# Layer 3 of a four-layer sequence: B from DRAM instead of TensorE, dt x spread in PSUM, C in banks of its own

## The chip, the cores and the metric

The kernel runs on one core of one Trainium2 chip. The metric is the device time of one launch in microseconds (us); lower is better. All arithmetic is float32.

## The reference, cut to what matters

Four layers follow one another on an image of 2 x 128 x 64 x 64: a two-way Mamba scan (layer 0), two attention layers (1 and 2), and the layer that is changed here. Layer 3 reads the 128 channels of each of the 8192 pixels as a short sequence of 8 tokens with 16 features, and runs a small Mamba over it (32 inner channels, 16 states), then a group norm, a Silu and a residual:

```python
seq = x.transpose(0, 2, 3, 1).reshape(B * H * W, 8, 16)
xi, z = split(seq @ in_proj_w.T, 2)              # 32 + 32 inner channels
xs = silu(causal_conv4(xi) + conv_b)
dt, Bm, Cm = split(xs @ x_proj_w.T, [1, 17])     # 1, 16 and 16 columns
dt = softplus(dt @ dt_proj_w.T + dt_proj_b)
dA = exp(dt[..., None] * A)
dBx = dt[..., None] * Bm[:, :, None, :] * xs[..., None]
h = dA_t * h + dBx_t                             # over the 8 tokens
y = (sum over states of h * C_t) + xs * D
xr = (y * silu(z)) @ out_proj_w.T
out = x + silu(group_norm(xr) * gamma + beta)
```

## The kernel before

The whole program is written out in order by hand, in one manual schedule per layer; every engine then runs its own queue in that order, waiting on semaphores only. Layer 3 begins at line 1090.

**Tiling.** The 2 x 4096 pixels are cut into 16 chunks of T = 512 pixels (eight for each image). Within a chunk the partitions hold 4 tokens x 32 inner channels, so two groups (index `i`) hold the 8 tokens; row block `j` of 32 partitions is one token. For the recurrence each token is spread out: partition 32 n + d holds channel d with four of the 16 states, and the remaining four groups `g` of states lie along the free axis. `PLACE` (line 39) tells in which `(i, j)` the two tokens of a step lie: a chunk takes four steps `k`, each with two tokens `o` = 0, 1. The first token of step 0 needs no decay and the last token of step 3 no state.

**What a step computes.**
- `dtr` (line 1216): dt of a token, spread over the states by transfers. The chunk's `put` writes dt and dt x to DRAM (`ddt`, `ddx`), and `spread(k)` reads them back with four transfers of 64 KB a token, into `dtr` and `rx`.
- `da_` (1253): A = exp(dt a), four ScalarE instructions, one for each `g`.
- `db_` (1245): TensorE spreads B over the partitions through `spread_by` with the weights `lb`, one matmul of 32 x 128 for each token and `g`, into a tile `q`; VectorE multiplies by `rx` into D.
- `mul` and `add` (1260, 1266): the recurrence. GpSimd forms A h in place of A; the sum D + A is the new h, in halves of two `g`, three of four halves on VectorE and one on GpSimd (`todo`).
- `hc_` (1271): TensorE spreads C with the weights `lc` into `q`, VectorE multiplies A h by it; `y_` (1285) sums the states on TensorE, with `y0_` (1277) having begun the sum with xs D and the part C·B dt x.

**What a chunk computes beside that.** `xs_`, `sz_`, `dt_` (1173 to 1188): projections of 1024 columns, two matmuls into one `q`. `e_exp`, `e_ln` (ScalarE), `dt_add`, `dtx_` (GpSimd): softplus and dt x. `bc_`, `cbx_` (1221, 1231): C·B for each token, spread and multiplied into dt x. `yg_`, `xr_`, `bn_`: gate, output projection, statistics. After eight chunks `Norm` treats the first image beside the next chunks.

**What sets the order.** The main loop goes over steps s and, in each, over four units g. In the body, `hc_` is of step s-1, the recurrence (`advance`) of step s, and `db_`, `da_` of step s+1; `extra` names what is put in at (k, g), such as the next chunk's projections, all one chunk ahead. This is the middle of it:

```python
for g in range(4):
    if pc_ is not None:
        pc_.hc_(pk, g)
    if g == 0:
        advance()
    if nc_ is not None:
        nc_.db_(nk, g)
    if g and pc_ is not None:
        pc_.y_(pk, g - 1)
```

**Buffers.** [...]`q` is a pair of banks with three buffers, shared by B, C and all projections, and `y` has two. D and A have three buffers each of (128, 2, 4, 512), `dtr` and `rx` two. All transfers go through SP's queue, in program order.

Of the kernel before, what the change touches and what calls it, by code (L numbers as in the profile page):

```python
# [13 lines left out]
P = 128  # L14
B, C, H, W = 2, 128, 64, 64
L = H * W
T = 512
# [4 lines left out]
NHC, NH, NDBU = 4, 3, 3  # L22
ND = 73
# [33 lines left out]
def conv_seq_kernel(ctx: ExitStack, tc: tile.TileContext, a: dict, out: bass.AP):  # L57
# [1031 lines left out]
    with ExitStack() as c3:  # L1089
# [8 lines left out]
        def pq():  # L1098
            return ps.tile([P, 2, T], F32, tag="q", name="q", bufs=3)
# [27 lines left out]
        lb = gt([P, NS, 32], "lb", wp)  # L1127
        lc = gt([P, NS, 32], "lc", wp)
        nc.vector.tensor_copy(lb, _bc(xpT[:, 1:17], 2, [P, NS, 32]))
# [17 lines left out]
        for b in range(B):  # L1147
            nc.sync.dma_start(kept[b], x[:, b, :])
# [6 lines left out]
        class Chunk3:  # L1155
# [10 lines left out]
            def two(self, w, rhs):  # L1166

                self.p = pq()
                for i in range(2):
                    mm(self.p[:, i, :], lhsT=w[:, i * P : (i + 1) * P] if w.shape[1] > P else w,  # L1170
                       rhs=rhs(i), start=True, stop=True)

            def xs_(self):
                self.two(flat(lm), lambda i: x[:, self.b, self.sl])
                self.xs = wt("xs", bufs=3)
                act(self.xs, self.p, AF.Silu, bias=v("cb3"))

            def sz_(self):
                self.two(flat(lz), lambda i: x[:, self.b, self.sl])
                self.sz = wt("sz", bufs=3)  # L1180
                act(self.sz, self.p, AF.Silu)

            def dt_(self):
                self.two(flat(ldt), lambda i: self.xs[:, i, :])
                self.e = wt("e")
                self.dt = wt("dt", bufs=1)
                act(self.e, self.p, AF.Abs, bias=v("bdt3"))
                nc.vector.tensor_scalar(self.dt, self.p, v("bdt3"), 0.0, ALU.add, ALU.max)
# [13 lines left out]
            def put(self):  # L1202
                self.ddt = dr.tile([P, 2, T], F32, tag="ddt", name="ddt")
                self.ddx = dr.tile([P, 2, T], F32, tag="ddx", name="ddx")
                nc.sync.dma_start(self.ddt, self.dt)
                nc.sync.dma_start(self.ddx, self.e)

            def spread(self, k):

                i, j = PLACE[k]  # L1210
                for what, src, toks in (("dtr", self.ddt, (1,) if k == 0 else (0, 1)),
                                        ("rx", self.ddx, (0,) if k == 3 else (0, 1))):
                    t = wt(what)
                    for n in range(4):
                        for o in toks:
                            nc.sync.dma_start(t[32 * n : 32 * n + 32, o, :],  # L1216
                                              src[32 * (j + o) : 32 * (j + o) + 32, i, :])
                    getattr(self, what)[k] = t


            def bc_(self):
                self.p = pq()
                for j in range(2):
                    for i in range(2):
                        mm(self.p[64 * i : 64 * i + 64, j, :], lhsT=flat(wbc[:, j]),
                           rhs=self.xs[:, i, :], start=True, stop=True)
                self.bs = wt("bs", (P, T), bufs=1)
                nc.scalar.copy(self.bs, self.p[:, 0, :])
                nc.vector.tensor_mul(self.bs, self.bs, self.p[:, 1, :])

            def cbx_(self):
                self.two(flat(nsum), lambda i: self.bs)
                nc.vector.tensor_mul(self.e, self.e, self.p)


            def spread_by(self, w, k, g, toks):
                i, j = PLACE[k]
                q = pq()
                for o in toks:
                    r = slice(32 * (j + o), 32 * (j + o) + 32)  # L1240
                    mm(q[:, o, :], lhsT=flat(w[r, 4 * g : 4 * g + 4, :]), rhs=self.xs[r, i, :],  # L1241
                       start=True, stop=True)
                return q[:, toks[0] : toks[-1] + 1, :]

            def db_(self, k, g):
                toks = (0,) if k == 3 else (0, 1)
                if g == 0:
                    self.D[k] = wt("D", (P, 2, 4, T), bufs=3)
                q = self.spread_by(lb, k, g, toks)
                sl = slice(toks[0], toks[-1] + 1)  # L1250
                nc.vector.tensor_mul(self.D[k][:, sl, g, :], self.rx[k][:, sl, :], q)  # L1251

            def da_(self, k, g):
                sl = slice(1, 2) if k == 0 else slice(0, 2)
                if g == 0:
                    self.A[k] = wt("A", (P, 2, 4, T), bufs=3)
                act(self.A[k][:, sl, g, :], self.dtr[k][:, sl, :], AF.Exp,  # L1257
                    scale=aneg[:, 2 * NS + g : 2 * NS + g + 1])

            def mul(self, k, o, half):  # L1260
                g = slice(2 * half, 2 * half + 2)
                h = self.D[k][:, 0, g, :] if o else self.D[k - 1][:, 1, g, :]
                a_ = self.A[k][:, o, g, :]
                nc.gpsimd.tensor_mul(a_, a_, h)  # L1264

            def add(self, k, o, half, eng):
                g = slice(2 * half, 2 * half + 2)
                d = self.D[k][:, o, g, :]
                eng.tensor_add(d, d, self.A[k][:, o, g, :])  # L1269

            def hc_(self, k, g):
                toks = (1,) if k == 0 else (0, 1)
                q = self.spread_by(lc, k, g, toks)
                a_ = self.A[k][:, toks[0] : 2, g, :]
                nc.vector.tensor_mul(a_, a_, q)  # L1275

            def y0_(self, i):
                if i == 0:
                    self.y = {}
                self.y[i] = ps.tile([P, T], F32, tag="y", name="y", bufs=2)  # L1280
                for w, rhs in ((diag_d, self.xs), (ident, self.e)):
                    mm(self.y[i], lhsT=w, rhs=rhs[:, i, :], start=w is diag_d, stop=False,  # L1282
                       skip_group_check=True)

            def y_(self, k, g):
                i, j = PLACE[k]
                for o in (1,) if k == 0 else (0, 1):
                    r = slice(32 * (j + o), 32 * (j + o) + 32)
                    mm(self.y[i][r], lhsT=rep[:, 0:32], rhs=self.A[k][:, o, g, :], start=False,  # L1289
                       stop=(g == 3 and k % 2 == 1), skip_group_check=True)  # L1290


            def yg_(self, i):
                nc.vector.tensor_mul(self.sz[:, i, :], self.sz[:, i, :], self.y[i])

            def xr_(self):
                self.p = pq()
                for i in range(2):
                    mm(self.p[:, 0, :], lhsT=flat(lo[:, i]), rhs=self.sz[:, i, :],
                       start=(i == 0), stop=(i == 1))  # L1300
                nc.scalar.copy(x[:, self.b, self.sl], self.p[:, 0, :])
# [4 lines left out]
        class Norm:  # L1306
# [3 lines left out]
            def first(self):  # L1310
                self.mv = wt("mv", (P, 2), bufs=1)
                nc.vector.bn_aggr(self.mv, flat(stats[:, self.b]))
                self.p = pq()[:, 0, :]
                mm(self.p[:, 0:1], lhsT=gmean, rhs=self.mv[:, 0:1], start=True, stop=True)

            def second(self):
# [8 lines left out]
                self.p = pq()[:, 0, :]  # L1325
# [17 lines left out]
            def load_all(self):  # L1343
                t = wt("D", (P, 2, 4, T), bufs=3).rearrange("p a g t -> p (a g t)")
                nc.sync.dma_start(t, kept[self.b])
                for k in range(4):
                    self.xl[k] = t[:, 1024 * k : 1024 * k + 1024]
# [14 lines left out]

        def at(s):
            return steps[s] if 0 <= s < len(steps) else (None, 0)

        with tc.manual_schedule():
            c = chunks[0]
            c.xs_()
            c.sz_()
            c.dt_()  # L1370
            c.e_exp()
            c.e_ln()
            c.dt_add()
            c.dtx_()
            c.put()
            for k in range(2):
                c.spread(k)
            c.bc_()
            c.cbx_()
            norms = [Norm(b) for b in range(B)]  # L1380
            for s in range(-1, len(steps) + 3):
                (pc_, pk), (cc, ck), (nc_, nk) = at(s - 1), at(s), at(s + 1)
                ci, k = divmod(s, 4)
                fut = chunks[ci + 1] if s >= 0 and ci + 1 < len(chunks) else None
                old = chunks[ci - 1] if ci > 0 else None
# [25 lines left out]
                extra = {}  # L1411

                def more(key, *what):
                    extra.setdefault(key, []).extend(what)

                if cc is not None:
                    more((0, 0), lambda: cc.y0_(0))
                    more((0, 4), lambda: cc.spread(3))
                    more((2, 2), lambda: cc.y0_(1))
                    more((3, 1), lambda: cc.yg_(0))  # L1420
                if old is not None:
                    more((1, 1), lambda: old.yg_(1))
                if fut is not None:
                    f = fut
                    more((0, 2), f.xs_)
                    more((0, 3), f.sz_)
                    more((1, 1), f.dt_, f.e_exp, f.e_ln)
                    more((1, 2), f.bc_)
                    more((1, 3), f.dt_add, f.dtx_, f.put)
                    more((1, 4), lambda: f.spread(0))  # L1430
# [164 lines left out]
```

## Time and profile before

| | |
|---|---|
| device time, three runs | 6737.71, 6741.09, 6753.5 us (median 6741.09) |
| the profiled execution | 6743.73 us; its span from first to last instruction 6741.9 us |
| layer 0 / layers 1 and 2 / layer 3 (page's slices and timeline) | to about 3.5 ms / to about 5.63 ms / from 5629 to 6742 us |
| chunks of layer 3 | 64.8 to 65.5 us for most; 75.5 and 75.4 us for the two beside which the first image is normalised |
| a steady chunk, busy us | TensorE 58.5, VectorE 51.8, GpSimd 49.0, ScalarE 26.9; DMA share 0.26, 73 GB/s |

How to read the profile's rows: a row of the timeline gives start and duration, the engine (PE is TensorE, PEld its weight loads, DVE VectorE, ACT ScalarE, POOL GpSimd, SPq the sync engine's queue of transfers), the line, the operation, the tile written and those read. In brackets stands how long the engine sat idle before it and who released it. A row of the waits view names who waited for whom. A row of groups gives busy us in all and mean ns of one. A float32 matmul of 512 columns is recorded as two passes, so counts of TensorE are double those in the code.

### The profile page before, as it was taken

How to read it: one execution, taken by the hardware profiler on the slowest of the kernel's cores; microseconds unless marked ns; L12 is line 12 of the kernel's file. 1: busy time of each engine (PE TensorE's matmuls, PEld its weight loads, DVE VectorE, ACT ScalarE, POOL GpSimd, SP SyncE). 2: the span in 40 equal slices, each digit the busy share in tenths (PEclk: the TensorE clock that was granted, in tenths of full speed). 3: DMA queues.
4: the chain of work that ended last, by engine and by line, in shares of the span. 5: the costliest groups of instructions: out<-in, count | busy, mean ns of one | idle time of the engine just before them, and what ended most of it. 6: DMA issues, size and time to landing. Idle time of an engine off the chain costs nothing. (4 is left out here: it accounts for less than half of the span.)

```text
span 6741.9 us, 67309 instructions
## 1 busy us (share of the span) xinstructions
PE 5957.8 (88%) x20652; PEld 2794.8 (41%) x20652; DVE 5535.0 (82%) x4521; ACT 4446.2 (66%) x7658; POOL 5393.9 (80%) x2471
## 2 busy tenths in 40 slices
PE   8888888888888888888889999999999997888888
PEld 2222222222222222222238877787788883222222
DVE  7999999999999999999986665565566676787777
ACT  7887788877788777887765654554456554434343
POOL 6999999999999999999975665555566666777676
PEclk7888788877778778787779999999999998888898
DMA  6656665665566665566620000000000002222222
GB/s 183 146 149 158 162 151 145 148 153 145 142 157 152 155 151 140 147 156 151 154 73 1 5 3 1 1 1 1 1 1 13 1 1 64 75 69 72 88 73 73
DMA packets 354733, 616.78 MB, mean 91 GB/s; under 512 B 73785, under 2 KB 76226, under 8 KB 353858
## 3 DMA queue, kind: packets, MB, share of 16 engines
q1 hardware_dynamic: 353488, 610.44, 35.9%
q8 instruction: 162, 2.65, 0.2%
q14 instruction: 201, 1.65, 0.1%
q10 hardware_dynamic: 882, 2.04, 0.1%
HBM read 496.72 MB, written 115.47 MB: 91 GB/s over the span
## 5 line engine op out<-in xcount | busy, mean ns | idle before, releaser
L383 POOL TENSOR_TENSOR dbu<-dus,bs 128x1024 f32<-128x1024 f32 x1024 | 2458.0, 2437 | 100.1 <-DVE h L427 85.5
L427 DVE TENSOR_TENSOR_SCAN h<-da,hst,dbu 128x1024 f32<-128x1024 f32 x896 | 2090.7, 2340 | 93.5 <-ACT dbu L411 88.8
L396 ACT ACTIVATE da<-dts,aneg 128x512 f32<-128x512 f32 (+1 forms) x2048 | 1410.1, 689 | 343.8 <-DVE h L427 305.5
L923 POOL TENSOR_TENSOR sum<-sum,sc 128x1024 f32<-128x1024 f32 x384 | 906.3, 2360 | 492.3 <-ACT sc L918 488.6
L885 ACT COPY sc<-s 128x512 f32<-128x512 f32 x1024 | 597.7, 585 | 858.8 <-PE s L880 745.1
L892 DVE TENSOR_TENSOR mx<-mx,s 128x512 f32<-128x512 f32 x896 | 609.1, 680 | 546.8 <-ACT sc L885 545.5
L880 PE MATMUL s<-q,k 128*128 128x256 f32 x4096 | 1051.6, 380 | 6.6 <-DVE k L857 3.3
L450 PE MATMUL y<-hc,cst 128*32 128x512 f32 x4096 | 880.2, 755 | 196.0 <-DVE hc L439 176.1
L935 PE MATMUL av<-sc,v 128*128 128x256 f32 x4096 | 1049.4, 379 | 2.5 <-ACT sc L918 2.5
L439 DVE TENSOR_TENSOR hc<-h,pc 128x1024 f32<-128x1024 f32 x704 | 841.4, 1195 | 9.7 <-PE y L450 7.4
L880 PEld LDWEIGHTS s<-q,k 128*128 128x128 f32 x4096 | 776.6, 190 | 140.3 <-issue 29.0
L935 PEld LDWEIGHTS av<-sc,v 128*128 128x128 f32 x4096 | 768.6, 190 | 103.1 <-ACT sc L918 3.9
L437 POOL TENSOR_TENSOR hc<-h,cs 128x1024 f32<-128x1024 f32 x320 | 762.0, 2381 | 1.1 <-issue 1.1
L1264 POOL TENSOR_TENSOR A<-A,D 128x1024 f32<-128x1024 f32 x224 | 525.6, 2363 | 231.7 <-DVE D L1269 202.5
L416 PE MATMUL pc<-xd,sel 16*128 16x512 f32 x1024 | 708.1, 782 | 0.1
L915 DVE TENSOR_TENSOR sc<-sc,pm 128x1024 f32<-128x1024 f32 x512 | 620.1, 1212 | 0.9 <-PE pm L911 0.9
L918 ACT ACTIVATE sc<-sc 128x1024 f32<-128x1024 f32 x512 | 541.9, 1059 | 8.6 <-DVE sc L915 8.1
L1257 ACT ACTIVATE A<-dtr,aneg 128x1024 f32<-128x1024 f32 (+1 forms) x256 | 245.8, 1031 | 389.4 <-PE y L1289 374.0
L340 PE MATMUL misc<-xd,w_dt 9*128 9x512 f32 x504 | 371.3, 824 | 145.0 <-ACT x L479 79.6
L450 PEld LDWEIGHTS y<-hc,cst 128*32 128x32 f32 x4096 | 125.3, 120 | 852.9 <-DVE hc L439 414.5
L1241 PE MATMUL q<-xs,lb 32*128 32x512 f32 x896 | 332.1, 713 | 75.4 <-DVE D L1251 68.6
L411 ACT ACTIVATE dbu<-hst,dbu,df 128x1 f32<-128x1 f32 x896 | 337.9, 377 | 82.5 <-POOL dbu L383 60.2
(263 smaller groups left out, 7868.4 us busy)
## 6 DMA issues: line engine op xcount, KB each, us to landing
dts<-ddt SPq DMA_DIRECT2D x512, 256.0 KB, 5.5
dus<-ddu SPq DMA_DIRECT2D x512, 256.0 KB, 5.1
bs<-rows SPq DMA_DIRECT2D x1024, 64.0 KB, 4.8
cs<-rows SPq DMA_DIRECT2D x1024, 64.0 KB, 3.3
ddt<-dt SPq DMA_DIRECT2D x128, 256.0 KB, 2.0
ddu<-dtu SPq DMA_DIRECT2D x128, 256.0 KB, 4.0
dtr<-ddt SPq DMA_DIRECT2D x448, 64.0 KB, 2.0
rx<-ddx SPq DMA_DIRECT2D x448, 64.0 KB, 2.0
```

The source lines that it names most:

```text
L383: nc.gpsimd.tensor_mul(t, self.dus[q], _bc(self.bs[g], 1, [P, 2, T]))
L396: act(t[:, i, sl], self.dts[q][:, i, sl], AF.Exp, scale=an[:, g, 2 * q + i : 2 * q + i + 1])
L416: mm(t, lhsT=sel[32:48, 4 * g : 4 * g + 4, :].rearrange("p n d -> p (n d)"), rhs=self.xd[32:48, :], start=True, stop=True)
L427: nc.vector.tensor_tensor_scan(ho, ai, bi, init, ALU.mult, ALU.add)
L437: nc.gpsimd.tensor_mul(t, self.h[u], _bc(self.cs[gq(u)[0]], 1, [P, 2, T]))
L439: nc.vector.tensor_mul(t, self.h[u], _bc(self.pc[u // 2], 1, [P, 2, T]))
L450: mm(self.y[q // 2][r : r + 32, :], lhsT=sum4, rhs=self.hc[u][:, i, :], start=False, stop=(u % 8 >= 6), skip_group_check=True)
L880: mm(p[:, o, :], lhsT=j.k[m // 8][:, m % 8 * P : m % 8 * P + P], rhs=self.q, start=True, stop=True)
L892: nc.vector.tensor_max(self.mx, self.s[0][:, 0:2, :] if u == 1 else self.mx, self.p[u])
L915: nc.vector.tensor_sub(s, s, _bc(self.pm[:, :], 1, [P, 4, NQ]))
L923: nc.gpsimd.tensor_add(self.sum, self.s[0] if w == 1 else self.sum, self.s[w])
L935: mm(self.av, lhsT=self.job.v[m // 8][:, m % 8, :], rhs=self.s[u // 2][:, m % 4, :], start=(m == 0), stop=(m == 31))
```

## The change

- **B by transfers.** `b_` copies the chunk's B rows (which `bc_` already made for C·B) to SBUF and stores them in DRAM (`rows`, 256 KB). `load(k, o)` fills D of one token (128, 4, 512) with B by four transfers of 256 KB, each reading four rows and repeating them over 32 partitions. D is now allocated for each token, in six half-size buffers. The weights `lb` go.
- **dt x by TensorE.** `rx_(k, o)` spreads a token's dt x over the partitions with one matmul into a PSUM bank (two buffers), instead of by transfers; the store `ddx` and the transfers to `rx` go. `db_` multiplies D in place by that bank, repeated over two `g`, in two halves a token.
- **C alone.** `pc_` makes C's tile `q` (two buffers of two banks), one unit ahead of the `hc_` that uses it (`prepare`). Step 0 of a chunk takes two units of 1024 columns instead of four of 512.
- **Projections in halves.** `xs_`, `sz_`, `dt_`, `cbx_` work on 512 columns each, through one bank `misc`; `xs_`, `sz_`, `b_`, `dt_` and `e_exp` are put two chunks ahead, the rest of the chain one chunk ahead. dt's relu moves from VectorE to ScalarE. C·B dt x is written over dt, not over dt x. `y` has one bank.
- **Copies of x.** The copy of each image's x to `kept` moves from before the loop to step 1 of chunks 0 and 1.

The diff, cut to its core:

```diff
+ND3 = 6
...
-        def pq():
-            return ps.tile([P, 2, T], F32, tag="q", name="q", bufs=3)
+        def misc():
+            return ps.tile([P, T], F32, tag="misc", name="misc")
...
-        for b in range(B):
-            nc.sync.dma_start(kept[b], x[:, b, :])
...
+            def one(self, w, rhs):
+                p = misc()
+                mm(p, lhsT=w, rhs=rhs, start=True, stop=True)
+                return p
+
+            def xs_(self, i):
+                if i == 0:
+                    self.xs = wt("xs", bufs=3)
+                p = self.one(flat(lm)[:, i * P : (i + 1) * P], x[:, self.b, self.sl])
+                act(self.xs[:, i, :], p, AF.Silu, bias=v("cb3"))
...
+            def b_(self):
+                p = self.bc_(0)
+                self.bs = wt("bs", (P, T))
+                nc.scalar.copy(self.bs, p)
+                self.rows = dr.tile([P, T], F32, tag="rows", name="rows")
+                nc.sync.dma_start(self.rows, self.bs)
+
+            def c_(self):
+                self.pc = self.bc_(1)
+
+            def cb_(self):
+                self.cb = wt("cb", (P, T), bufs=1)
+                nc.vector.tensor_mul(self.cb, self.bs, self.pc)
+
+            def dt_(self, i):
...
+                p = self.one(flat(ldt), self.xs[:, i, :])
+                act(self.e[:, i, :], p, AF.Abs, bias=v("bdt3"))
+                act(self.dt[:, i, :], p, AF.Relu, bias=v("bdt3"))
...
+            def load(self, k, o):
+
+                if k == 3 and o:
+                    return
                 i, j = PLACE[k]
+                t = self.D[k, o] = wt("D", (P, 4, T), bufs=ND3)
+                r = 64 * i + 16 * (j + o)
+                src = self.rows[r : r + 16].rearrange("(g n) t -> n g t", n=4)
+                for n in range(4):
+                    nc.sync.dma_start(t[32 * n : 32 * n + 32], src[n].partition_broadcast(32))
+
+            def cbx_(self, i):
+                self.pcb = self.one(flat(nsum)[:, i * P : (i + 1) * P], self.cb)
+
+            def ecb_(self, i):
+                nc.vector.tensor_mul(self.dt[:, i, :], self.e[:, i, :], self.pcb)
+
+            def rx_(self, k, o):
...
+                q = self.rx[k, o] = ps.tile([P, T], F32, tag="rx", name="rx", bufs=2)
+                mm(q, lhsT=rep[r, :], rhs=self.e[r, i, :], start=True, stop=True)
+
+            def db_(self, k, o, half):
+                d = self.D[k, o][:, 2 * half : 2 * half + 2, :]
+                nc.vector.tensor_mul(d, d, _bc(self.rx[k, o], 1, [P, 2, T]))
...
+            def unit(self, k, u):
+
+                return [(1, 2 * u), (1, 2 * u + 1)] if k == 0 else [(0, u), (1, u)]
+
+            def pc_(self, k, u):
+                i, j = PLACE[k]
+                self.q = getattr(self, "q", {})
+                q = self.q[k, u] = ps.tile([P, 2, T], F32, tag="q", name="q", bufs=2)
...
                 if cc is not None:
-                    more((0, 0), lambda: cc.y0_(0))
-                    more((0, 4), lambda: cc.spread(3))
-                    more((2, 2), lambda: cc.y0_(1))
-                    more((3, 1), lambda: cc.yg_(0))
+                    more((1, 2), lambda: cc.y0_(0), at=first)
+                    more((3, 2), lambda: cc.y0_(1), at=first)
+                    more((3, 0), lambda: cc.yg_(0))
...
+                if fut2 is not None and s >= 0:
+                    more((2, 1), lambda: fut2.xs_(0))
+                    more((2, 2), lambda: fut2.xs_(1))
+                    more((2, 3), lambda: fut2.sz_(0))
+                if fut2 is not None:
+                    more((3, 0), lambda: fut2.sz_(1), at=first)
+                    more((3, 1), fut2.b_)
+                    more((3, 2), lambda: fut2.dt_(0))
+                    more((3, 3), lambda: fut2.dt_(1), fut2.e_exp)
                 if fut is not None:
...
+                    more((0, 0), fut.e_ln)
+                    more((0, 1), fut.c_)
+                    more((0, 2), fut.cb_, fut.dt_add, fut.dtx_)
+                    more((0, 3), fut.put)
+                    more((0, 3), lambda: fut.cbx_(0))
+                    more((1, 0), lambda: fut.ecb_(0), lambda: fut.cbx_(1))
+                    more((1, 1), lambda: fut.ecb_(1))
+                if 0 <= ci < B:
+                    more((1, 3), lambda: nc.sync.dma_start(kept[ci], x[:, ci, :]))
+                if n2 is not None:
+                    more((k, 1), lambda: n2.load(n2k, 0))
+                    more((k, 2), lambda: n2.load(n2k, 1))
+                    more((k, 3), lambda: n2.spread(n2k))
+                    more((k, 2), lambda: n2.rx_(n2k, 0), at=first)
+                if nc_ is not None:
+                    more((k, 0), lambda: nc_.rx_(nk, 1), at=first)
...
                 for g in range(4):
+                    if g < units:
+                        prepare()
+                    if g == 0 and older is not None and ok:
+                        older.y_(ok, 3)
+                    for f_ in first.get((k, g), []):
+                        f_()
+                    for u in sums.get(g, []):
+                        pc_.y_(pk, u)
+                    if g < units:
+                        pc_.hc_(pk, g)
+                    if nc_ is not None and nk != 3:
+                        nc_.db_(nk, g // 2, g % 2)
+                    elif nc_ is not None and g % 2 == 0:
+                        nc_.db_(nk, 0, g // 2)
                     if g == 0 and nc_ is not None:
-                        for gg in range(4):
-                            nc_.da_(nk, gg)
-                    if g in (1, 2):
+                        nc_.da_(nk)
+                    if g < 3:
                         advance()
                     for f_ in extra.get((k, g), []):
                         f_()
```

Here `n2` is the step after next (s+2), `fut2` the chunk after next, and `first` holds what goes ahead of a unit's sums.

## The prediction

> **What bounds the kernel now.** I read the page's slices first: the last seven carry layer 3 (5629 us to the end), and the diff touches nothing else. Then the windows view, cut at the load of the Silu table that opens each chunk of 512 tokens' work (columns: us, busy us of TensorE, its weight loads, VectorE, ScalarE, GpSimd, clock, DMA share, GB/s):
>
> ```profile
> 5794.77:5859.64 64.87, 58.50 (x206) 15.11 (x208) 51.83 (x47) 26.93 (x28) 48.97 (x21) 0.89 0.25 73
> 5859.64:5924.52 64.88, 58.52 (x206) 15.09 (x208) 51.86 (x47) 26.92 (x28) 48.99 (x21) 0.89 0.26 73
> ```
>
> A steady chunk takes 64.9 us and no engine fills it; TensorE is nearest. So the waits view of 5650 to 6740 us (engine and line that waited, for whom, us in total, times, longest):
>
> ```profile
> POOL A L1264 <- DVE D L1269: 202.5, 82, 8.4
> PEld q L1241 <- DVE D L1251: 173.5, 101, 7.8
> DVE A L1275 <- PE q L1241: 138.9, 100, 3.1
> ...
> PE q L1241 <- DVE D L1251: 90.2, 39, 7.0
> ...
> DVE D L1269 <- POOL A L1264: 45.8, 17, 5.8
> POOL dt L1197 <- ACT e L1194: 45.7, 15, 6.3
> ```
>
> TensorE and VectorE wait for each other: the three buffers of q are shared by B, C and the projections, B's matmul waits for VectorE's last product, and VectorE (138.9/16 = 8.7 us a chunk) waits for C's. GpSimd hangs behind: its product waits for VectorE's sum. ScalarE's largest wait, 374 us for y, is slack.
>
> A second limit shows in the timelines, VectorE first, then GpSimd (start, us):
>
> ```profile
> 6156.46 3.35 DVE L1269 TENSOR_TENSOR D<-D,A 128x1024 f32<-128x1024 f32 x1 [2.24 <-POOL A L1264]
> ...
> 6173.29 2.98 DVE L1269 TENSOR_TENSOR D<-D,A 128x1024 f32<-128x1024 f32 x1
> ```
> ```profile
> 6154.07 4.66 POOL L1264 TENSOR_TENSOR A<-A,D 128x1024 f32<-128x1024 f32 x2
> ...
> 6170.51 4.68 POOL L1264 TENSOR_TENSOR A<-A,D 128x1024 f32<-128x1024 f32 x2 [1.25 <-DVE D L1269]
> 6175.27 3.22 POOL L1269 TENSOR_TENSOR D<-D,A 128x1024 f32<-128x1024 f32 x1
> ```
>
> The sum issued at 6156.46 ends 1.1 us after GpSimd's products (6158.73); the one at 6173.29 ends 1.08 us after 6175.19, and GpSimd's next operation then takes 3.22 instead of 2.36 us. They take turns.
>
> **What the Trainium skill says.** "SBUF — State Buffer", section "SBUF: two separate sides": a VectorE operation with two SBUF inputs and a GpSimd operation hold one shared port pair exclusively; an operand from PSUM doesn't need it, nor do DMAs. The trace agrees: sums take 1.21 to 3.37 us, the products with q (L1251, L1275) never over 1.22. "TensorEngine Tiling (Array Packing)", "Key Properties": tiles run in parallel. Agrees: B and C in different rows overlap here (start, us):
>
> ```profile
> 6130.26 0.70 PE L1241 MATMUL q<-xs,lc 32*128 32x512 f32 x2
> 6130.27 0.70 PE L1241 MATMUL q<-xs,lb 32*128 32x512 f32 x2
> ```
>
> "TensorE: Matmul & The Clock Gate", Part 1: the clock drops after about 3.4 us of idling. Agrees: after 3.56 us idle at 6160.47 two passes last 2.07 us where back-to-back passes take 0.59.
>
> **The change, part by part, for one chunk.** One matmul of 512 columns is recorded as two passes, 0.98 us from start to start (L1170: two matmuls in 1.98); a pair in different rows or columns takes about 1.0 (L1289 x4: 6127.36 to the next at 6128.35).
>
> *TensorE.* Now C is 16 units (12 pairs, 4 singles), B 16, y 16; the rest is 5 x 1.95 (xs, sz, dt, B·C spread, output) + 2.9 (B and C rows, L1225) + 2 x 2.1 (y0) = 16.9. Laid end to end that is 64.9; the 58.5 busy say that 6.4 of B lie over C. The change removes B's 16 and adds 7 matmuls that spread dt x (nearest row: a single of L1241, 1.0). So 16 + 16 + 7 + 16.9 = 55.9. The gain is **2.6, not 9**. If three of the seven overlap C in other rows it is 53.
>
> *VectorE.* B x dt x becomes 14 products of 1024 by a spread PSUM row instead of 12 x 1.21 + 4 x 0.68. The layer has no such form; layer 0 has, at 1195 ns:
>
> ```profile
> L439 DVE TENSOR_TENSOR hc<-h,pc 128x1024 f32<-128x1024 f32 x704 | 841.4, 1195 | 9.7 <-PE y L450 7.4
> ```
>
> I take 1.21; the ends are 1.19 and 1.28 (L1188). 14 x 1.21 = 16.9 against 17.2; C's products likewise 16.9 against 17.3; dt's relu (1.28) moves to ScalarE; B·C's product splits, 1.36 for 1.21. Together -1.8: 51.8 becomes 50.
>
> *ScalarE.* Three 1024-wide reads of PSUM in halves and two relus: from the 0.58 of a 512-wide copy (L1228), +1.5 on 26.9. Nothing while the wait for y is its largest; but the projections now share one bank (misc), so a late ScalarE would stop TensorE. Table loads stay four a chunk.
>
> *GpSimd and the shared ports.* Work is unchanged, but exponent and logarithm come earlier, so the 45.7/15 = 3 us wait of L1197 goes; what is late next is VectorE's sum. Port time: 18 x 2.34 + 2.85 + 2.35 + 8 sums x 1.1 = 56.1 a chunk, before and after.
>
> *SP and DMA.* Issues stay 58 a chunk (28 for dt, 28 for dt x or B, 2 stores) at 0.45 us (x8 in 3.56). Bytes rise from 4.7 MB to 28 x 64 KB + 28 x 256 KB + 0.8 MB = 10 MB, or 165 GB/s. Layer 0 carries 140 to 183 GB/s at a DMA share of 0.6, with pieces of this size:
>
> ```profile
> dts<-ddt SPq DMA_DIRECT2D x512, 256.0 KB, 5.5
> ```
>
> B is asked for one step (about 15 us) before its product. Its six half-buffers come free as the preceding step ends, so I cost it at nothing; the cover is that step. SP waits in order: the store of dt waits for GpSimd, with spreads and B loads behind it, as today (14 us a chunk at L1205); ScalarE's exponent waits for the spread. Two waits are new: VectorE's B product for its tile's four transfers, with C's product and a sum queued behind it and TensorE and GpSimd waiting for those; and the product that overwrites dt, early in step 1, for dt's store, issued late in step 0 and landing in 2.6 us (DMA view, ddt<-dt of 512 KB). The second hides behind two products and a sum. The copies of x (2 MB, 6.3 us) move from the start to steps 1 and 5, where B loads queue behind them: 0 to 6 us each, taken as offset by the start they leave.
>
> *Order.* C is made one unit ahead in two banks, so VectorE no longer waits for the matmul it has just released. The compiled order then gives each of a chunk's four steps (TensorE, in us):
>
> step 0: C 5, y 4, dt x 2, C rows 1.45, one B·C spread 1: 13.4
> step 1: C 3, y 5, dt x 2, spread 1, y0 2.1, output 1.95: 15.0
> step 2: C 4, y 3, dt x 1, xs 2, one z 1: 11.0
> step 3: C 4, y 4, dt x 2, z 1, y0 2.1, B rows 1.45, dt 1.95: 16.5
>
> The ports: step 0 two products and a sum of GpSimd's (3 x 2.34), 5.2 for dt, one sum of VectorE's (1.1), 13.3; steps 1 and 2 five of GpSimd's and three sums, 15.0; step 3 five and one, 12.8. VectorE, at 1.13 a product from start to start, 1.9 a sum, 0.6 a small one: 11.5, 14.3, 13.1, 11.5. The largest of each sum to 59.9. Lookahead of one unit can't carry step 2's slack far into step 3; I add 0.5 for turns at the ports: **60.4 against 64.9**. Times 15 (the sixteenth chunk is split over a start and an end that gain nothing: the start puts three more matmuls ahead, the end is unchanged; -5 to +6) gives 68 us. 6741.9 - 68 = 6674 of span; 1.8 us lie around it, and the profiled run stands 2.6 above the median: 6673.
>
> **The rivals.**
> - *The full gain.* Steps smooth over and the ports alone bind, 57 a chunk: -7.9 x 16 = -126, 6615. For it: clocks near 0.97 when TensorE never idles (5470 to 5629 us). Against: ports 98% full.
> - *Nothing.* Product, sum, product of the recurrence already sets the time, and TensorE's waits only fill it: chunks of 64 to 65.5, 6727 to 6750. For: GpSimd's 202.5 us wait for sums. Against: those sums stand behind products that wait for TensorE.
> - *Slower: transfers.* As compiled, each transfer of SP waits for the one eight places before it, so 58 of mean landing time L need 58 L/8. At the 2 us of today's 64 KB that is 15 us; at 5.5, 40; **from L = 9 it exceeds 64.9**. At 10 a chunk takes 72.5: +7.6 x 16 = +122, 6863. For: layer 0's pieces land in up to 7.5 us, and B's tile holds four. Against: its median.
> - *It doesn't do what it says*: if B's product waits for its tile each time, TensorE's gap remains under another name; this is the transfers' case in small.
>
> **How the numbers follow.** Forecast 0.56 (58.5 to 63 a chunk, 6640 to 6711), full gain 0.13, nothing 0.11, slower 0.20. About 0.3%, 20 us, is what a measurement of this kernel can tell from no change; "nothing" gives 0.02 to faster, 0.07 to same and 0.02 to slower, and 0.01 of the forecast's tail goes to same. Faster 0.70, same 0.08, slower 0.22. The range 6610 to 6765 takes in forecast, full gain, nothing and the mildest of slower; beyond it lie about 0.05 below and 0.15 above.
>
> **What would show it.** Right: chunks near 60 us; VectorE's wait for C's matmul well under 2 us a chunk; TensorE busy about 56 at a clock over 0.92; sums still 1.9 on average or more; DMA share near 0.6; the 3 us wait of L1197's successor gone. Wrong: waits of VectorE's B product or ScalarE's exponent for DMAs of over 2 us a chunk, pieces landing in over 9 us, or GpSimd's wait for sums staying near 12 us a chunk.

## The result, and the profile after

The changed kernel takes 6790.75 us (median of 6 runs, 6786.51 to 6801.13) against 6739.23 for the kernel before in the same comparison: a ratio of 1.0079, 95% interval 1.0065 to 1.0092. It is slower by 0.8%; 6673, 1% faster than before, had been forecast.

Where the time went is read from two marks: GpSimd's last addition of the layers ahead (L958 before, L959 after), and ScalarE's copy of a chunk's result (L1301 before, L1325 after), one a chunk. These are the addition and the first copy before, then after:

```profile
5628.50 0.73 POOL L958 TENSOR_TENSOR x<-x,t 128x256 f32<-128x256 f32 x1 [4.15 <-ACT t L956]
5756.48 0.59 ACT L1301 COPY x<-q 128x512 f32<-128x512 f32 x1 [3.56 <-PE q L1299]
5623.71 0.73 POOL L959 TENSOR_TENSOR x<-x,t 128x256 f32<-128x256 f32 x1 [4.14 <-ACT t L957]
5793.27 0.59 ACT L1325 COPY x<-misc 128x512 f32<-128x512 f32 x1 [10.15 <-PE misc L1323]
```

The layers ahead are the same in all kernels, but end between 5616 and 5634 us in the profiles of this case, so layer 3 is timed from that addition. From it to the first copy it is 128.0 us before and 169.6 after: 42 more at the start. From the first copy to the fourteenth it is 877.3 and 894.0 us: 17 more for 13 chunks, 68.8 a chunk on average instead of 67.5. From there to the end it is 108.1 and 112.0: 4 more. Layer 3 is 62 us longer in the profiled execution, whose earlier layers ended 5 us sooner; between the medians it is 52.

The windows view of the changed kernel, cut as before at the load of the Silu table (columns as before), shows two chunks:

```profile
5868.31:5935.78 67.47, 55.17 (x165) 14.46 (x162) 53.05 (x43) 28.65 (x32) 48.75 (x21) 0.87 0.62 148
5935.78:6006.65 70.87, 59.08 (x165) 15.35 (x162) 53.75 (x43) 28.66 (x32) 49.81 (x21) 0.83 0.60 141
```

TensorE, costed at 55.9 us, is busy 55.2 in the first of these and 59.1 in the second, at clocks of 0.87 and 0.83; GpSimd's work stayed, and yet the chunk is longer. No engine is as full as TensorE was before (82 and 83% here, 90% then). The waits view, 5650 to 6800 us, names other pairs than before:

```profile
POOL dt L1217 <- ACT e L1214: 206.7, 16, 31.3
...
PEld misc L1165 <- DVE dt L1251: 166.7, 17, 14.0
PE misc L1165 <- DVE dt L1251: 150.4, 17, 12.5
...
ACT L1271 <- DMA dtr<-ddt: 133.1, 15, 10.3
DVE D L1283 <- POOL A L1278: 130.9, 46, 7.5
POOL A L1278 <- DVE D L1283: 101.1, 62, 4.6
...
DVE A L1300 <- PE q L1295: 55.7, 35, 5.9
...
DVE D L1265 <- DMA D<-rows: 31.1, 20, 8.8
```

VectorE's wait for C fell from 138.9 to 55.7 us, as meant, and GpSimd's for VectorE's sums from 202.5 to 101.1. But GpSimd now stands 206.7 us at L1217, the softplus sum, for ScalarE's logarithm; before it was 45.7. (31.3 of the 206.7 is the first chunk's, whose wait lies ahead of the window before.) And VectorE waits 130.9 for GpSimd, where it was 45.8.

One chunk shows the order of these waits. First SP's queue of the changed kernel (start, us of the group):

```profile
5882.66 0.34 SPq L1193 DMA_DIRECT2D rows<-bs  x1
5883.11 3.73 SPq L1244 DMA_DIRECT2D D<-rows  x8
5887.07 8.56 SPq L1232 DMA_DIRECT2D dtr<-ddt  x8
```

Then ScalarE, GpSimd, VectorE and TensorE in the same chunk:

```profile
5892.05 1.06 ACT L1211 ACTIVATE e<-e 128x1024 f32<-128x1024 f32 x1
5898.75 4.27 ACT L1271 ACTIVATE A<-dtr,aneg 128x1024 f32<-128x1024 f32 x4 [5.65 <-DMA D<-rows]
5903.04 1.28 ACT L1214 ACT_TABLE_LOAD   x1
5904.33 1.06 ACT L1214 ACTIVATE e<-e 128x1024 f32<-128x1024 f32 x1
```
```profile
5905.47 2.34 POOL L1217 TENSOR_TENSOR dt<-dt,e 128x1024 f32<-128x1024 f32 x1 [12.62 <-ACT e L1214]
```
```profile
5912.56 3.35 DVE L1283 TENSOR_TENSOR D<-D,A 128x1024 f32<-128x1024 f32 x1 [7.32 <-POOL A L1278]
5916.42 0.67 DVE L1251 TENSOR_TENSOR dt<-e,misc 128x512 f32<-128x512 f32 x1
```
```profile
5917.15 2.07 PE L1165 MATMUL misc<-cb,nsum 128*128 128x512 f32 x2 [10.91 <-DVE dt L1251]
```

Read from top to bottom: the B loads and the spread of dt for step 1 of the next chunk leave SP only after the store of the rows, at 5883. The spread's last pieces are issued at 5895, because each waits for one of the B pieces ahead of it. ScalarE, free since 5893, starts the exponents at 5898.75; the logarithm of the chunk after stands behind them; GpSimd waits 12.62 us for it, with the products of step 1 queued behind; VectorE's first sum waits 7.32 for such a product; TensorE's second C·B spread waits 10.91 for VectorE, and then takes 2.07 us for its two passes, which at 5901.17 took 1.12 (the windows view has a clock of 0.53 for 5917 to 5925).

SP's own waits say how long the store holds the queue, 302.7/15 = 20 us a chunk:

```profile
SPq L1193 <- ACT bs L1191: 302.7, 15, 27.6
SPq L1232 <- DMA D<-rows: 158.4, 203, 1.7
```

### The profile page after: what moved, and what is told of

It is laid out like the page before. It is cut to its first block, busy times and chain, and to the rows that moved or that the text cites. A ratio compares the mean times of both kernels' runs of the same rounds, so it can differ in the third digit from the quotient of the medians.

```text
span 6799.3 us, 66250 instructions
## 1 busy us (share of the span) xinstructions
PE 5964.9 (88%) x19980; PEld 2797.7 (41%) x19980; DVE 5548.7 (82%) x4456; ACT 4472.3 (66%) x7737; POOL 5378.7 (79%) x2471
## 5 line engine op out<-in xcount | busy, mean ns | idle before, releaser
L1278 POOL TENSOR_TENSOR A<-A,D 128x1024 f32<-128x1024 f32 x224 | 523.9, 2358 | 129.9 <-DVE D L1283 101.1
L1283 DVE TENSOR_TENSOR D<-D,A 128x1024 f32<-128x1024 f32 x128 | 282.6, 2208 | 130.9 <-POOL A L1278 130.9
L1295 PE MATMUL q<-xs,lc 32*128 32x512 f32 x896 | 301.8, 687 | 36.0 <-DVE A L1300 35.9
```

## The experiments

**The theories.** Theory 1: two queues are in the wrong order for this structure. SP's store of the B rows (put in at step 3, unit 1) stands ahead of step 3's loads and spread, which don't need it; and ScalarE's logarithm stands behind four exponents from which it needs nothing. Theory 2: the transfers' rate is the limit. Theory 3: the single bank `misc` holds TensorE up.

All ratios are to the kernel before, which ran beside each; the changed kernel's is 1.0079. In the expectations, e1 to e10 are the runs in the order in which they stand here.

### The store of the rows behind the spread

The store leaves `b_` and becomes a function of its own, `rows_` (cut, comments added):

```diff
-                nc.sync.dma_start(self.rows, self.bs)     # in b_, at (3, 1)
+                if fut2 is not None:
+                    more((3, 3), fut2.rows_)              # after n2.spread
```

> Only the place of the store of the B rows in SP's queue changes: behind step 3's B loads and spread of dt (unit 3) instead of ahead of them (unit 1). Theory 1 (SP stands at that store until ScalarE has copied the rows, 20 us a chunk, so the loads and the spread for step 1 of the next chunk are issued late, ScalarE's exponent and logarithm wait, GpSimd's softplus sum stands 12.6 us, VectorE and TensorE behind it): chunks fall from 67.5 to about 61, ScalarE's wait for dtr from 8.9 us a chunk to under 2, time 6670 to 6705. Theory 2 (rate of transfers: 148 GB/s and landing times of 5.9 us are the limit whatever the order): 6780 to 6800. Theory 3 (the single misc bank holds TensorE up): 6775 to 6800.

Measured: 6739.01 us, ratio 0.9993 (0.9983 to 1.0003). 0.9% of the time is back, with not a byte less to carry, so theory 2 falls; but the forecast of 6670 to 6705 is missed as well. SP's wait at the store fell from 302.7 to 79.7 us. But its wait for the softplus sum, at the store of dt, rose from 114.4 to 227.2 us, and ScalarE's wait for step 2's dt, whose spread stands behind that store, stayed (133.1, now 129.9) where the expectation had it fall. In step 1 the spread now is in time, and still the logarithm comes late. ScalarE and GpSimd in one chunk of this kernel:

```profile
5946.77 1.05 ACT L1213 ACTIVATE e<-e 128x1024 f32<-128x1024 f32 x1
5947.72 4.26 ACT L1273 ACTIVATE A<-dtr,aneg 128x1024 f32<-128x1024 f32 x4
5952.00 1.28 ACT L1216 ACT_TABLE_LOAD   x1
5953.29 1.06 ACT L1216 ACTIVATE e<-e 128x1024 f32<-128x1024 f32 x1
```
```profile
5954.43 2.36 POOL L1219 TENSOR_TENSOR dt<-dt,e 128x1024 f32<-128x1024 f32 x1 [6.87 <-ACT e L1216]
```

The exponents start without a wait at 5947.72, and GpSimd stands 6.87 us all the same: 4.26 for them, the rest for the table and the logarithm. The order in ScalarE's queue is a cost of its own.

### The logarithm ahead of the exponents

```diff
-                    more((0, 0), fut.e_ln)
+                    more((0, 0), fut.e_ln, at=first)
```

> Only ScalarE's order changes: in step 0 the logarithm of the next chunk goes ahead of the exponents of step 1, so that it doesn't stand behind their wait for dtr; the transfers stay as they are. Theory 1: GpSimd's 12.6 us wait shrinks to under 4, the store of dt goes out 7 us sooner, but step 1's exponents still come late; chunks 61 to 64, time 6700 to 6745. Theory 2 and theory 3: no change, 6775 to 6800.

Measured: 6707.85 us, ratio 0.9953 (0.9937 to 0.997), in the stated range and faster than before. Most chunks take 60.2 to 63 us. GpSimd's wait for the logarithm falls from 206.7 to 87.5 us (31.3 of each is the first chunk), while SP still stands 246.4 us at the store of the rows. One move of one instruction turns a loss of 0.8% into a gain of 0.5%.

### Two banks for misc

```diff
-            return ps.tile([P, T], F32, tag="misc", name="misc")
+            return ps.tile([P, T], F32, tag="misc", name="misc", bufs=2)
...
-                q = self.rx[k, o] = ps.tile([P, T], F32, tag="rx", name="rx", bufs=2)
+                q = self.rx[k, o] = ps.tile([P, T], F32, tag="rx", name="rx", bufs=1)
```

> misc gets two banks and the dt x spread one (eight banks in all, as before). Theory 3: TensorE's 20 us a chunk of waiting at the second C·B spread goes, 6700 to 6740. Theory 1: that wait is only where the late softplus arrives at TensorE; it moves to the next instruction, and the single bank for dt x adds a little: 6780 to 6815. Theory 2: 6780 to 6800.

Measured: 6989.87 us, ratio 1.0371 (1.0349 to 1.0393), far outside all three ranges. The bank taken from dt x costs more than a second one for the projections could bring: TensorE stood 214 us at the spread of dt x for VectorE's last product by it, and VectorE 330.8 us for C, queued behind that spread. So this run doesn't judge theory 3; it says that dt x needs its two banks. As the cause of the loss, theory 3 falls with a later run: with both queues mended and `misc` unchanged the kernel is faster than before, and TensorE's weight loads wait 40.3 us for VectorE's C·B product instead of 166.7. What the single bank still costs there, no run shows.

### The spread of dt ahead of the B loads

```diff
-                    more((k, 1), lambda: n2.load(n2k, 0))
+                    more((k, 1), lambda: n2.spread(n2k), lambda: n2.load(n2k, 0))
...
-                    more((k, 3), lambda: n2.spread(n2k))
```

> In every step the spread of dt goes ahead of the B loads in SP's queue, the store of the rows stays where it was (ahead of both in step 3). Theory 1: dtr for step 1 lands about 8 us sooner (4 us of issues and 4 us of waiting for B's pieces before it), so the exponents, the logarithm and GpSimd come sooner; B's tiles land 4 us later and VectorE's product waits 2 to 4 us for them: chunks 62 to 65, 6705 to 6760. Theory 2: the same bytes at the same rate, 6780 to 6800. Theory 3: 6775 to 6800.

Measured: 6780.91 us, ratio 1.0061 (1.0046 to 1.0076): at the lower end of theory 2's range and inside theory 3's, 21 us above the upper end of theory 1's. What the earlier spread brings, the later B tiles take: GpSimd's wait for the logarithm falls from 206.7 to 137.2 us, but VectorE's product waits 82 us for B, up from 31.1, and GpSimd 156.6 for VectorE's sums, up from 101.1. With the store of the rows ahead of both, turning round the two behind it moves most of the wait and doesn't end it.

### Both orders mended

The edits of the first two runs together.

> Both reorderings together: the store of the B rows behind step 3's loads and spread (as in e1), and the logarithm ahead of step 1's exponents (as in e2). Theory 1 (two queues hold GpSimd's softplus sum: SP's through dtr, ScalarE's through its order; e1 lifted the first, e2 went round it): GpSimd's wait for the logarithm under 2.5 us a chunk, ScalarE's waits for dtr under 2, chunks 59.5 to 61, and some 10 us at the start because step 1's loads no longer wait for the second chunk's rows: 6670 to 6695. Rival (the rate of transfers takes over once the order is mended): chunks stay at e2's 61 to 63, 6695 to 6715.

Measured: 6659.01 us, ratio 0.9875 (0.986 to 0.989), faster than theory 1's range. Two of the chunks (windows view), and GpSimd's wait for the logarithm:

```profile
5950.40:6008.62 58.22, 54.91 (x165) 14.40 (x162) 53.20 (x43) 28.66 (x33) 49.44 (x20) 0.94 0.73 172
6008.62:6066.77 58.15, 54.83 (x165) 14.46 (x162) 53.14 (x43) 28.65 (x32) 49.43 (x20) 0.94 0.72 172
```
```profile
POOL dt L1219 <- ACT e L1216: 74.6, 16, 31.3
```

They take 58.2 us each, with nearly the same busy times and the same bytes as the changed kernel's 67 to 71, at 172 instead of some 148 GB/s. From the last addition ahead of the layer to the first copy it is 147.0 us: about half of the 42 lost at the start is back. Here too both orders count: of the 22.5 us the store alone had brought 10.5, the logarithm alone 6. The rival, that the rate takes over, is refuted.

Between this run and the changed kernel lie 132 us. The logarithm's move brings 83 of them if it comes first and 80 if it comes second, the store's 52 or 49. So the two costs add up, and ScalarE's order is the larger.

### The start

The first chunk's projections are made 1024 columns at a time in the tiles of `q`, which stand idle then; its B loads go ahead of dt's store and the first spread of dt x ahead of C·B's:

```diff
-            for i in range(2):
-                c.xs_(i)
+            p = pair(flat(lm), lambda i: x[:, c.b, c.sl])   # two matmuls into one q
+            c.xs = wt("xs", bufs=3)
+            act(c.xs, p, AF.Silu, bias=v("cb3"))
...
+            c.load(0, 0)
+            c.load(0, 1)
             c.dt_add()
             c.put()
...
+            c.rx_(0, 0)
             for i in range(2):
                 c.cbx_(i)
                 c.ecb_(i)
```

> e5, and layer 3's lead-in written with the idle two-bank tiles of q for the first chunk's projections (1024 columns at once, instead of one bank at a time with ScalarE in between), B loads ahead of dt's store, and the first spread of dt x ahead of C·B's. Theory: the start of the changed kernel costs some 30 us against before (first output copy at 5793 against 5756), about half of it in single-bank turns of 2.8 us each and waits behind them: 15 to 25 us below e5, 6650 to 6675. Rival: the start is set by the chain of softplus and transfers alone: within 6 us of e5.

Measured: 6648.08 us, ratio 0.9864 (0.9847 to 0.9881). That is 11 us under the run before, below the 15 expected and within the two intervals of each other: after the start of the layer, the first softplus sum comes 10 us sooner than in the run before, and the first copy only 2 (145.4). The single-bank turns were not the main cost of the start; what makes up the other 17 us against the kernel before isn't shown. No later run is clearly faster than this one.

### C·B dt x in a tile of its own

This edit and the last two stand on top of the run of the start.

```diff
-                nc.vector.tensor_mul(self.dt[:, i, :], self.e[:, i, :], self.pcb)
+                if i == 0:
+                    self.ex = wt("ex")
+                nc.vector.tensor_mul(self.ex[:, i, :], self.e[:, i, :], self.pcb)
...
-                for w, rhs in ((diag_d, self.xs), (ident, self.dt)):
+                for w, rhs in ((diag_d, self.xs), (ident, self.ex)):
```

dt and the B rows go from two buffers to one, so that the new tile has room.

> e6, and C·B dt x goes to a tile of its own instead of over dt, so that VectorE's product in step 1 needn't wait for dt's store (dt and the B rows get one buffer each to make room). Theory: in e2 VectorE stood 2.0 us there and TensorE 4.3 us behind it, at a lower clock for 8 us after; if that remains in e6, 1 to 2 us a chunk go, 15 to 30 us below e6. Rival: recurrence and shared ports set the chunk; within 8 us of e6.

Measured: 6651.15 us, ratio 0.9864 (0.9849 to 0.9879), the same as without. TensorE's weight loads wait 35.6 us for that product, 33.6 without the edit. With the softplus in time, the store of dt isn't what the product waits for: without the edit, that wait is 0.4 us in all.

### The spread ahead of the loads, with the orders mended

The edit of the fourth run on top of the fifth, both orders mended.

> e5 with the spread of dt ahead of the B loads in every step. Theory 1: with the order mended, dtr isn't what any chain waits for; within 8 us of e5 either way. Rival (dt's pieces waiting in line behind B's, each for the transfer eight places before it, still hold ScalarE up): 15 us or more below e5.

Measured: 6667.19 us, ratio 0.9891 (0.9874 to 0.9909) against 0.9875 (0.986 to 0.989): 8 us above the fifth run, at the edge of theory 1's "within 8 us", with intervals that overlap. The rival's 15 us or more of gain are refuted: that dt's pieces are issued behind B's costs nothing that can be seen once SP is free in time.

### Every B transfer twice

```diff
-                for n in range(4):
+                for n in (0, 1, 2, 3, 0, 1, 2, 3):
```

> e6 with every B transfer issued twice into the same tile (16.6 MB a chunk instead of 10). Theory (rate has slack at one time's bytes, DMA share 0.72 in chunks of 58.2 us, but not at two): the share would have to be 1.2, so transfers bind; 86 transfers through eight places at 6.5 to 8 us each are 70 to 86 us a chunk, 6840 to 7090. Rival (the six half-buffers and a step of lead hide even that): within 20 us of e6's 6648.

Measured: 6980.11 us, ratio 1.0334 (1.0317 to 1.0352), in the range of the theory. Five chunks and a bit of this kernel in the windows view (its DMA share and GB/s are the last two columns), and its row in the DMA view:

```profile
5900.00:6300.00 400.00, 301.63 (x841) 77.44 (x841) 252.46 (x217) 149.81 (x167) 252.58 (x103) 0.83 0.98 221
```
```profile
D<-rows SPq DMA_DIRECT2D x896, 256.0 KB, 4.7
```

At 221 GB/s the transfers' share is 0.98: that is the ceiling for this mix of pieces, and the mended kernel's 172 at 0.72 lies below it. A chunk takes 79 us. The landing time of a piece, 4.7 us at the median, is no longer than in the changed kernel (5.9).

### All sums on VectorE

```diff
-                            cc.add(ck, o, hf, V if w == "v" else G)
+                            cc.add(ck, o, hf, V)
```

> e6 with GpSimd's quarter of the recurrence's sums on VectorE. Theory A (turns at the shared ports and GpSimd bind a mended chunk at 58.2): port time falls by 4 x 1.24 = 5 us a chunk, chunks 55 to 57.5, 6605 to 6640. Theory B (VectorE, busy 53.2 of 58.2, binds): four more sums of 1.2 to 2.2 us lengthen it, chunks 60 to 65, 6675 to 6750.

Measured: 6658.56 us, ratio 0.986 (0.9844 to 0.9876), the same as with GpSimd's quarter (0.9864), between the two theories' ranges. The chunks say more than the total. These two follow each other, from one copy of the result to the next:

```profile
5837.02:5892.40 55.38, 52.88 (x163) 13.77 (x163) 53.47 (x46) 28.65 (x32) 36.25 (x16) 0.97 0.75 177
5892.40:5957.29 64.89, 60.79 (x163) 15.06 (x164) 58.98 (x49) 28.66 (x32) 41.13 (x18) 0.84 0.71 171
```

Of the 13 chunks between the first copy and the fourteenth, eight take 55.4 to 57.2 us, as theory A forecast; two take 64.9, at a clock of 0.84, in theory B's range. The 13 together take 768 us, against 772 in the run of the start, and what follows takes 8 more. So with fewer operations on GpSimd an undisturbed chunk is shorter than 58.2, which speaks for GpSimd and the ports as its limit, though the clock is higher there too (0.97 against 0.94); what makes the long chunks isn't shown. A sum of VectorE's is shorter on average, but there are more of them, and GpSimd's wait for them doubled, from 89.8 to 176.8 us. VectorE's rows of groups in this kernel, then in the one of the start, 5700 to 6600 us:

```profile
L1285 DVE TENSOR_TENSOR D<-D,A 128x1024 f32<-128x1024 f32 x181 | 311.7, 1722 | 5.1 <-POOL A L1280 5.1
```
```profile
L1285 DVE TENSOR_TENSOR D<-D,A 128x1024 f32<-128x1024 f32 x123 | 269.9, 2194 | 38.9 <-POOL A L1280 38.9
```

The mean of a sum falls from 2194 to 1722 ns when GpSimd has fewer operations of its own, as turns at the ports would have it; and VectorE, with four more sums, is busy 53.5 us in the short chunk, about as before (53.2).

## Why the prediction was wrong, step by step

Two steps failed, both on what stands ahead of an instruction in its queue: the first and the third of these points. The third cost 80 to 83 us, the first 49 to 52.

- **"SP waits in order: the store of dt waits for GpSimd, with spreads and B loads behind it, as today." This step failed: it left out a wait.** The part counted two stores a chunk and gave the wait of one. The other, of the B rows, waits for ScalarE and stands in step 3 ahead of the loads and spread for step 1. It held SP 20 us a chunk. The Trainium skill, "DMA: Bandwidth & Descriptors", section "Anatomy of one DMA — SWDGE (gpsimd) path", says that DMA engines don't wait on semaphores: the wait is at the issuing sequencer, before dispatch. The trace agrees, with the rows of 5882.66 and 5883.11: eight loads whose data had long been there left with the store.
- **"B is asked for one step (about 15 us) before its product ... the cover is that step."** That was reasoned from the buffers alone. For step 1 of a chunk the loads left at 5883 and VectorE stood ready for the first product that needed them at 5890: half a step, not one. That product itself waited little (31.1 us in all, 2 a chunk). But the eight spreads behind the loads took 8.56 us to issue instead of about 3.6.
- **"... exponent and logarithm come earlier, so the 45.7/15 = 3 us wait of L1197 goes." This step failed, and cost the most.** The exponential does come earlier, two chunks ahead. The logarithm was put behind step 1's four exponents in ScalarE's queue, and the wait became (206.7 - 31.3)/15 = 11.7 us. With step 1's transfers in time 6.87 remain in the chunk that the first experiment showed. The compiled order had been worked through for TensorE, VectorE and the ports, and not for ScalarE's queue, where GpSimd's wait begins.
- **"-5 to +6" for the start** was +42: the first chunk's step 1 waits for the second chunk's rows, and its logarithm stands behind the exponents, too. With both orders mended it is +19; rewriting the start takes 2 of these. The rest stays open.
- **The rival "Slower: transfers"** got the sign and not the mechanism. Its price was 58 L/8 for a landing time L, deciding at 9 us. L was 5.9 for B and 4.7 for dt, which with the two stores is 38 us a chunk. With every B transfer doubled the formula gives 48 (56 at 4.7, 28 at 3.9, two stores), and the chunk took 79: the eight places were not the limit then either, the rate was.
- **What held.** With the two queues mended a steady chunk is 58.2 us where the sum of the four steps gave 60.4: TensorE 54.9 busy (55.9 costed) at a clock of 0.94 (over 0.92 expected), VectorE's products by a spread PSUM row 1210 ns (1.21 taken), sums 2.2 us on average (1.9 or more), ScalarE 28.65 (28.4), and the port time as costed, 56.1, still below it. "What would show it" named, for wrong, ScalarE's exponent waiting over 2 us a chunk for DMAs, which is what came.
- **What missed beside that.** VectorE is busy 53.2 us, not 50, mostly because its sums take longer than before (2.2 us, 1.9 then). Its wait for C, forecast well under 2 us a chunk, is 3.4 even with the queues mended (54.3 us in all).
- **Luck.** The mended kernel's 6659 is 14 us from the 6673 forecast for the changed one. But it gains 6.7 us a steady chunk, not 4.5, and its start loses 19, not 6 at most: two errors that cancel in part. The gain was there, and the orders of SP's and ScalarE's queues took it back with 52 us on top.

That the first and the third of these points, SP's order and ScalarE's, make up the loss is shown by the runs that mended one, the other and both. What binds the mended chunk at 58.2 us is not settled; the last run's short chunks speak for GpSimd and the ports.

## What to carry to other kernels

When a change adds a transfer to a queue, list what stands behind it there and who makes its data: a store that waits for a late engine holds back loads that need nothing. Do the same for every engine's queue that an edit moves an instruction into, not only for the engine that is fullest: here a logarithm behind four exponents on ScalarE, busy 42% of the chunk, idled GpSimd. And before a structure is given up because it came out slower, look at whether its busy times came out as costed; if they did, the loss is in the waits, and a change of order alone may end them.

## What the runs showed of the hardware that had not been expected

- Pieces of 256 KB made of 2 KB rows, each row repeated over 32 partitions, reached 221 GB/s (other pieces included) at a DMA share of 0.98, and a piece then landed in 4.7 us, sooner than at 148 GB/s in the changed kernel (5.9). So the landing time of a piece did not show here how near the transfers were to their limit; the share did.
- TensorE, after 10.91 us idle, needed 2.07 us for two passes, and 7.6 us went by before two passes took 1.12 again (5917.15 to 5924.76). So long an idle time isn't needed: in the run of the start, with both orders mended, these two rows stand in one chunk:

```profile
5897.65 1.13 PE L1297 MATMUL q<-xs,lc 32*128 32x512 f32 x4 [1.88 <-DVE A L1302]
5924.22 2.07 PE L1165 MATMUL misc<-cb,nsum 128*128 128x512 f32 x2 [1.09 <-DVE dt L1253]
```

After 1.88 us idle TensorE ran on at full speed; after 1.09 it began a stretch of 7 us at a clock of 0.52 (5924 to 5931), and the same came one chunk later (5982 to 5989). So the drop after about 3.4 us of idling, with which the prediction explained a row of before, isn't the whole of it; what starts such a stretch, no run shows.
